# Output projection with stationary weights and 256 moving tokens; a second layer that takes turned sums

## The chip, the core and the metric

The kernel is one program on one core of a Trainium2 chip. TensorE (PE) multiplies matrices, VectorE (DVE), ScalarE (ACT) and GpSimd (POOL) work on elements, and SyncE (SP) issues the transfers (DMA). Every engine takes its instructions in order from a queue of its own, and waits where one needs what another engine or a transfer has not yet done. The metric is the device time in microseconds; lower is better. A measurement of a kernel here is the median of several runs.

## The reference

Input x is 4 x 256 tokens of 512 columns in float32, handled as 1024 tokens. It goes through three layers, each added to x:

```python
x = L0_attn_hidden_states
x = x + 0.5 * _L0_ffn_ref(_layernorm(x, axis=-1), L0_ffn_A, L0_ffn_B, L0_ffn_Wr)
x = x + _L0_attn_ref(_layernorm(x, axis=-1), L0_attn_wq, L0_attn_wkv, L0_attn_wo)
x = x + 0.5 * _L0_ffn_ref(_layernorm(x, axis=-1), L0_ffn_A, L0_ffn_B, L0_ffn_Wr)
```

The attention has 32 heads and causal softmax, and ends in an output projection by `wo` (4096 x 512):

```python
attn = jnp.einsum('bhqk,bkhd->bqhd', probs, v).reshape(B, S, H * DV)
return jnp.einsum('bse,ed->bsd', attn, wo)
```

The feed-forward layer has 64 small experts of rank 16. Each token is routed to 16 of them:

```python
scores = xf @ Wr.T
top_vals, top_idx = jax.lax.top_k(scores, TOPK)
gates = jax.nn.softmax(top_vals, axis=-1)
G = jnp.zeros((N, K), xf.dtype).at[jnp.arange(N)[:, None], top_idx].set(gates)
h = jnp.einsum('nd,krd->nkr', xf, A)
out = jnp.einsum('nkr,kdr->nd', h * G[:, :, None], B)
```

The layernorm is (x − mean) / sqrt(var + 1e-5), with no weights. The same A, B and Wr serve both feed-forward layers.

## The kernel before

All products are in float32, which TensorE does as two records of the trace for each matmul instruction. To save products, every large matrix product is made by a scheme of Strassen's kind: a 2 x 2 block product is done with seven products (M1 to M7) instead of eight, of which four need sums of blocks on either side; the results are then added together. `left_sums` (L197) forms the left blocks' sums, `seven` runs the products with their reads.

Stages in order of time: the first feed-forward layer, the attention (16 groups p of two heads, eight units of one head and one batch each), the output projection, the second feed-forward layer "f2". x stays in SBUF throughout as a tile of 128 partitions x 8 token tiles x 512 columns, token within the tile on the partition.

**The projection** (`out_products`, L1312) uses the scheme on two levels. The outer one has seven products in the order M1, M2, M6, M5, M3, M7, M4, each in four parts of the inner dimension: 28 steps k. A step has 14 products, the seven inner ones for each of two groups g. For every k `load` (L1384, L1385) has SP fetch four raw blocks of the left operand (`ol`, attention outputs turned so that the inner dimension is on the partitions; 512 KB for each g) and of the right one (`or`, weights; 256 KB for each g), mostly three steps ahead; `sums` (L1391) forms the others on VectorE, four adds of 128x512 and four of 128x256; then each product is two matmuls of 128x128 (L1491), with 128 tokens stationary and 128 columns of the weights moving. A PSUM tile thus holds tokens on the partitions and columns along the free dimension. Steps 0 and 3 use operands held in pieces of their own (`o`). After every fourth step `read` (L1424, and one ACT copy, L1426) puts the seven accumulators together into `y` (seven adds of 128x256) and adds that, or a running `yu`, into the quarters of x (adds of 128x1024).

The projection's first products are spread among the last head groups' units; the driver at the end (from L1868 on) takes the rest one product at a time, 392 in all. At every 28th from 112 on it loads one of f2's seven `a` blocks, and at products 316 and 356 it lets f2 do a piece of its preparation.

**f2** goes over four pairs of token tiles. For a pair, `prepare` (L458) takes the layernorm's statistics (L111, L112), the root on ACT and the reciprocal on VectorE (L116, L117), normalizes on ACT (L137, `xn`), turns both tiles by eight TensorE transposes (L144, `ptx`), copies them to SBUF on ACT (L467, `fxT`), forms the four left sums (L197, `fxs`), makes the router's products (L367, `pr`) and the gates (`gate_of_one`, L431 to L455). `hidden` (L490, `ph`) makes h by seven products, read by L503 and L507 into `hg`; GpSimd multiplies by the gates (L521). `move` turns hg of the first three pairs in 32x32 blocks on VectorE (L534), sends the blocks through DRAM (L539, four DMAs for each of two tiles) and loads them back (L545); `turned` copies the result (ACT, L559) and forms the sums (VectorE, L570, `hs`). The last pair is turned by TensorE (L585). `back` (L604, `po`) makes the layer's output by seven products, and its reads (L616) add it to x; the store to DRAM is L1883. The loop runs hidden of pair u and then back of pair u − 1, with the preparation of pair u + 1 between.

Before the attention's end, each engine's order is written out by a list of due times (`written`, `later`), in units of TensorE's time. From the driver on, the order within each engine is set by a scheduler at build time from the program's order and dependences.

Of the kernel before, what the change touches and what calls it, by code (L numbers as in the profile page):

```python
# [14 lines left out]
P = 128  # L15
# [19 lines left out]
def macaron_kernel(  # L35
# [69 lines left out]
    def norm_stats(ts, name, whole=True):  # L105
# [3 lines left out]
        for j, t in enumerate(ts):  # L109
            st = small.tile([P, nc.vector.BN_STATS_DIM], F32, tag="st", name=f"st_{name}_{t}")  # L110
            tc.keep_in_program_order(nc.vector.bn_stats(out=st, in_=x[:, t, :]))  # L111
            nc.vector.bn_aggr(out=mv[:, j, :], in_=st)  # L112
# [188 lines left out]
    def ffn(name, pairs, a_sums, b_sums, after, late, aside=None, raw=None):  # L301


        with ExitStack() as scope:
# [123 lines left out]
            def gate_of_one(n, ps):  # L428

                sc = work.tile([P, E], F32, tag="sc", name=f"sc_{n}")  # L430
                nc.vector.tensor_copy(sc, ps[:, 0:E])  # L431
                top = work.tile([P, 8], F32, tag="top", name=f"top_{n}")
                nc.vector.max(out=top, in_=sc)
                left = work.tile([P, E], F32, tag="left", name=f"left_{n}")
                nc.vector.match_replace(
                    out=left, in_to_replace=top, in_values=sc, imm_value=TAKEN
                )
                top2 = work.tile([P, 8], F32, tag="top2", name=f"top2_{n}")
                nc.vector.max(out=top2, in_=left)
                left2 = work.tile([P, E], F32, tag="left2", name=f"left2_{n}")  # L440
                nc.vector.match_replace(
                    out=left2, in_to_replace=top2, in_values=left, imm_value=TAKEN
                )
                nmax = work.tile([P, 1], F32, tag="nmax", name=f"nmax_{n}")
                nc.vector.tensor_scalar_mul(nmax, top[:, 0:1], -1.0)
                ex = ps[:, E : 2 * E]
                nc.scalar.activation(ex, sc, AF.Exp, bias=nmax)
                gate = work.tile([P, E], F32, tag="gate", name=f"gate_{n}", bufs=4)
                den = work.tile([P, 1], F32, tag="den", name=f"den_{n}")
                nc.vector.scalar_tensor_tensor(  # L450
                    gate, left2, TAKEN, ex, ALU.is_equal, ALU.mult, accum_out=den
                )
                rden = work.tile([P, 1], F32, tag="rden", name=f"rden_{n}")
                nc.vector.reciprocal(rden, den)
                nc.scalar.mul(gate, gate, rden)  # L455
                return gate

            def prepare(pair):  # L458


                n = f"{name}_{pair[0]}"
                tokens = normed(work, pair, name)
                yield
                xt = work.tile([P, 2, DC, P], F32, tag="fxT", name=f"fxT_{n}")
                pt = [turned_x(tokens[i], f"{name}_{t}") for i, t in enumerate(pair)]
                for i in range(2):
                    nc.scalar.copy(xt[:, i], pt[i])  # L467
                xs = work.tile([P, 4, 2, P], F32, tag="fxs", name=f"fxs_{n}")
                left = left_sums(
                    nc.vector,  # L470
                    [xs[:, i] for i in range(4)],
                    *(xt[:, i, k : k + 2] for i in range(2) for k in (0, 2)),
                    pt[0][:, 0:2],
                    pt[0][:, 2:4],
                    xt[:, 1, 0:2],
                    pt[1][:, 2:4],
                )
                lefts.append(left)
# [3 lines left out]
                gated_by.append([gate_of_one(f"{name}_{t}", ps) for t, ps in zip(pair, scores)])  # L482
# [115 lines left out]
            def back(pair, left, b_right):  # L598
# [14 lines left out]
                def read(r, ps):  # L613
                    i, j, _ = READS[r]
                    to = x[:, pair[i], j * 256 : (j + 1) * 256]
                    nc.vector.tensor_tensor(to, to, ps[:, 0:256], ALU.add)  # L616
# [135 lines left out]
            else:  # L752
                tokens = ready(pairs[0])
                take(tokens, 1)
                yield
                take(tokens, 1)
                yield
                take(tokens, 1)
                a_right = a_sums()
            for u in () if late else range(n + 1):  # L760
                hid = hidden(pairs[u], lefts[u], hgs) if u < n else iter(())
                tokens = ready(pairs[u + 1]) if u + 1 < n else iter(())
# [3 lines left out]
                take(tokens, 1)  # L766
                take(hid, 2)
                take(tokens, 1)
                take(hid, 1)
                take(tokens, 1)  # L770
# [9 lines left out]
                if u < n:  # L780
                    gated(hgs[pairs[u]], gated_by[u], False)
                    if pairs[u] in by_dma:
                        take(move(pairs[u], hgs[pairs[u]]), 3)
                if u > 0:
# [242 lines left out]
    work = right_pool(attention, "work")  # L1027
    pairs = right_pool(attention, "pairs")
# [283 lines left out]
    def out_products():  # L1312
# [81 lines left out]
        def operand(k, n, g, t):  # L1394

            cols = slice(t * P, (t + 1) * P)
            if k in (0, 3):
                parts = tiles[k, g]
                return parts[t][:, L_AT[n]], parts[2][:, R_AT[n]]
            left, right = tiles[k]  # L1400
            return left[:, g, L_AT[n], cols], right[:, g, R_AT[n]]

        def block(i, j):
            return x[:, 4 * i : 4 * i + 4, j * 256 : (j + 1) * 256]

        def read(m, banks):

            if m == "M1":
                y = outer["pool"].tile([P, 4, 256], F32, tag="u", name="yu", bufs=1)
                outer["u"] = y  # L1410
            else:
                y = outer["pool"].tile([P, 4, 256], F32, tag="y", name=f"y_{m}", bufs=1)
# [545 lines left out]
```

## Time and profile before

| | us |
|---|---|
| median of 3 runs | 1111.73 (1111.62 to 1112.86) |
| the profiled execution, its own time | 1112.9 |
| its span | 1111.1 |
| granted TensorE clock | 1.0 |
| TensorE idle before, in the projection from 866.5 on | 0 |
| product L1491, records, busy | 1456, 165.0 |
| multiplications by the gates L521 on POOL, busy | 34.0 |
| start of the projection's last stretch on TensorE | 981.80 |
| end of the projection on TensorE (start of the router's products) | 997.88 |

The times of the trace count from the start of the span. A group of instructions stands under its source line, engine, operation and tile, with the number of records after an x. The duration of a single matmul record includes its latency, since matmuls overlap; what one costs in a full stream is read from the distance of two groups' starts. The chain of waits follows the last instruction back from cause to cause. The DMA issues have the median time from issue to landing.

### The profile page before, as it was taken

Reading aid. Unit: us, or ns where it says so; the run is one execution under the profiler, and the core shown is the slowest. Engines: PE = TensorE matmul, PEld = TensorE weight load, DVE = VectorE, ACT = ScalarE, POOL = GpSimd, SP = SyncE. Lnnn points to the kernel's source line nnn. Section 1 sums busy time; section 2 is a strip of 40 time slices with the busy share of each in tenths; the row PEclk is TensorE's granted clock in tenths of the full one; section 3 lists DMA queues with packets and bytes.
Section 4 is the critical chain, followed back from the end, with each engine's and each line's share of the span. In section 5 each row is a group of like instructions: output and inputs, shape, how many; then the busy total and the mean of one; then the engine's idle time right before and its main releaser. Section 6 shows DMA issues by size and latency. Waiting matters only on the chain.

```text
span 1111.1 us, 20951 instructions
## 1 busy us (share of the span) xinstructions
PE 1098.3 (99%) x6742; PEld 968.0 (87%) x6742; DVE 823.4 (74%) x2238; ACT 427.6 (38%) x1306; POOL 631.4 (57%) x877
## 2 busy tenths in 40 slices
PE   8999999999999999999999999999999999999998
PEld 5776888899999999999999999999899999995667
DVE  6655776778778778778778778878778978866543
ACT  2234334444544544544544544544442000106410
POOL 3935587737887887797788788788532000002120
PEclk9999999999999999999999999999999999999999
DMA  9412121057757656656756656755798998752331
GB/s 314 183 32 83 32 65 30 18 147 206 199 147 202 198 142 186 207 152 177 211 147 189 202 149 183 201 163 164 215 315 304 343 342 259 257 193 76 95 95 39
DMA packets 204638, 190.55 MB, mean 171 GB/s; under 512 B 74224, under 2 KB 166384, under 8 KB 204272
## 3 DMA queue, kind: packets, MB, share of 16 engines
q1 hardware_dynamic: 204528, 189.21, 56.5%
q8 instruction: 54, 0.88, 0.3%
q14 instruction: 56, 0.46, 0.1%
HBM read 119.28 MB, written 69.86 MB: 170 GB/s over the span
## 4 chain that ended last, share of the span: by engine, by line
PE 86%; DVE 5%; DMA 4%; POOL 3%; ACT 1%; issue 1%; SPq 1%; POOLq 0%; DVEq 0%
PE po_M L1491 12%; PE pqk_c L1067 9%; PE pqk_b L1067 8%; PE po_f L604 8%; PE pqk_d L1067 7%; PE ph_f L490 7%; PE pv_c L1166 5%; PE ps L1516 5%; PE pa L1592 4%; PE pqk_a L1067 4%; PE pv_b L1166 4%; PE ps L1515 2%; PE pa L1599 2%; PE pv_d L1166 2%; PE pv_a L1166 2%; PE pv_e L1166 2%
## 5 line engine op out<-in xcount | busy, mean ns | idle before, releaser
L521 POOL TENSOR_TENSOR hg_f<-hg_f,gate_f 128x512 f32<-128x512 f32 x32 | 34.0, 1078 | 232.9 <-ACT gate_f L455 151.8
L1491 PE MATMUL po_M<-or_M,ol_M 128*128 128x128 f32 x1456 | 165.0, 275 | 0.7 <-DVE or_M L1391 0.7
L1491 PEld LDWEIGHTS po_M<-or_M,ol_M 128*128 128x128 f32 x1456 | 163.8, 192 | 1.0 <-DVE or_M L1391 0.9
L911 POOL TENSOR_TENSOR wqk_M<-wqk_M 128x128 f32<-128x128 f32 x320 | 142.3, 459 | 12.1
L911 POOL TENSOR_TENSOR wqk_M<-wqk_M,wqk_M 128x512 f32<-128x512 f32 (+1 forms) x64 | 107.2, 1685 | 46.4 <-DMA wqk_M<-in_wkv 25.1
L1084 DVE TENSOR_TENSOR qk<-qk,pqk_d 128x512 f32<-128x512 f32 x210 | 116.3, 558 | 21.9 <-PE pqk_d L1067 18.0
L1536 ACT ACTIVATE s<-s,least 128x128 f32<-128x128 f32 (+1 forms) x256 | 114.1, 448 | 41.2 <-DVE least L1524 38.0
L1554 ACT ACTIVATE pn<-s,arden 128x128 f32<-128x128 f32 x220 | 94.0, 427 | 47.8 <-DVE arden L1545 43.2
L1067 PE MATMUL pqk_c<-xop,wqk_M 128*128 128x256 f32 x448 | 111.4, 380 | 0.1
L1067 PE MATMUL pqk_d<-xop,wqk_M 128*128 128x256 f32 x420 | 108.2, 381 | 1.1 <-DVE qk L1084 1.1
L1067 PE MATMUL pqk_b<-xop,wqk_M 128*128 128x256 f32 x420 | 102.9, 379 | 0.0
L1391 DVE TENSOR_TENSOR ol_M<-ol_M 128x512 f32<-128x512 f32 x104 | 75.9, 730 | 23.5 <-DMA ol_M<-left 21.9
L1524 DVE CUSTOM_DVE_ANT_0 s<-ps,mask 128x128 f32<-128x128 f32 (+1 forms) x256 | 80.8, 353 | 16.1 <-PE ps L1516 12.4
L1084 DVE TENSOR_TENSOR qk<-qk,pqk_c 128x256 f32<-128x256 f32 (+1 forms) x112 | 59.4, 531 | 40.5 <-PE pqk_c L1067 36.5
L1084 DVE TENSOR_TENSOR qk<-qk,pqk_b 128x512 f32<-128x512 f32 x105 | 71.3, 679 | 20.7 <-PE pqk_b L1067 19.9
L1067 PEld LDWEIGHTS pqk_c<-xop,wqk_M 128*128 128x128 f32 x448 | 79.1, 191 | 8.7 <-ACT qk L1116 1.2
L1606 ACT COPY attn<-pa 128x256 f32<-128x256 f32 x128 | 47.5, 371 | 99.5 <-PE pa L1599 86.6
L1067 PEld LDWEIGHTS pqk_b<-xop,wqk_M 128*128 128x128 f32 x420 | 74.9, 191 | 7.5
L1067 PEld LDWEIGHTS pqk_d<-xop,wqk_M 128*128 128x128 f32 x420 | 73.0, 191 | 9.1 <-DVE qk L1084 2.9
L1592 PE MATMUL pa<-pT,vbuf 128*128 128x256 f32 x256 | 76.4, 380 | 1.5 <-DMA pT<-moved 1.0
L1516 PE MATMUL ps<-qk 128*128 128x256 f32 x256 | 76.5, 380 | 0.0
L911 POOL TENSOR_TENSOR wv_M<-wv_M 128x128 f32<-128x128 f32 x160 | 71.5, 461 | 5.0 <-DMA wv_M<-in_wkv 0.6
(221 smaller groups left out, 2344.1 us busy)
## 6 DMA issues: line engine op xcount, KB each, us to landing
ol_M<-left SPq DMA_DIRECT2D x52, 512.0 KB, 5.8
moved<-s SPq DMA_DIRECT2D x440, 48.0 KB, 1.8
pT<-moved SPq DMA_DIRECT2D x110, 192.0 KB, 2.9
wv_M<-in_wkv SPq DMA_DIRECT2D x64, 128.0 KB, 2.6
wqk_M<-in_wq SPq DMA_DIRECT2D x64, 128.0 KB, 2.3
wqk_M<-in_wkv SPq DMA_DIRECT2D x64, 128.0 KB, 2.5
wo<-in_wo SPq DMA_DIRECT2D x16, 512.0 KB, 4.7
left<-attn SPq DMA_DIRECT2D x16, 512.0 KB, 3.3
```

What stands on the lines that cost most here:

```text
L490: nc.tensor.matmul(ps, lhsT=left[m][:, c, :], rhs=a_right[m][:, c, :], start=first and c == 0, stop=c == 1, skip_group_check=True,)
L604: nc.tensor.matmul(ps[:, 0:256], lhsT=left[m][:, c, :], rhs=b_right[m][:, c, :], start=first and c == 0, stop=c == 3, skip_group_check=True,)
L911: return nc.gpsimd.tensor_tensor(to, a, b, ALU.subtract)
L1067: nc.tensor.matmul(ps[:, i * S : (i + 1) * S], lhsT=right[m][n], rhs=xop[OUTER[m]][:, INNER[n]], start=first and i == 0, stop=True, skip_g ...
L1084: nc.vector.tensor_tensor(to, of, ps, ALU.add)
L1166: nc.tensor.matmul(ps[:, i * S + t * P : i * S + (t + 1) * P], lhsT=xop[OUTER[m]][:, INNER[n], t * P : (t + 1) * P], rhs=right[m][n], star ...
L1491: nc.tensor.matmul(banks[at // 2][:, cols : cols + P], lhsT=lhsT, rhs=rhs, start=k % 4 == 0 and g == 0 and at % 2 == 0 and t == 0, stop=Tr ...
L1516: nc.tensor.matmul(ps[:, P : 3 * P], lhsT=qT[:, P : 2 * P], rhs=kT, start=True, stop=True)
L1524: nc.vector.tensor_tensor_reduce(out=s[:, cols], in0=ps[:, cols], in1=mask_f[:, cols], scale=-SCALE, scalar=-TAKEN, op0=ALU.add, op1=ALU.m ...
L1536: nc.scalar.activation(s[:, cols], s[:, cols], AF.Exp, bias=least[:, i : i + 1], scale=-1.0, accum_out=den[:, i : i + 1],)
L1554: nc.scalar.mul(pn[:, :, i : 2 * i + 1, :].rearrange("p k t c -> p t k c"), s[:, cols].rearrange("p (t k c) -> p t k c", k=4, c=32), rden[ ...
L1592: nc.tensor.matmul(po[:, 0 : 2 * P], lhsT=v_of(p, j, 2 * b), rhs=of[:, 0:2], start=True, stop=False,)
```

## The change

Four things are changed.

1. In the projection, for all steps but 0 and 3, one product is one matmul with the right operand (weights, 128 columns) stationary and all 256 tokens moving. Steps 0 and 3 keep two matmuls of 128x128, with the sides exchanged as well. The accumulators then hold columns on the partitions and tokens along the free dimension, so `read` adds turned blocks.
2. So that these blocks can be added to x, the tokens of x are turned in 32x32 blocks in the attention stage: `turn_tokens`, once for each of the eight token tiles, in unit 1 of groups 2 to 9. VectorE transposes 128x512, four DMAs of 64 KB go out to DRAM and one of 256 KB comes back into x, on SP, at two due times.
3. `prepare` of f2 turns x back to plain tokens for the statistics and the later addition (`xp`, by a VectorE transpose of 128x1024, four DMAs of 128 KB and a load of 512 KB), takes the statistics of `xp`, sends the means to DRAM as a row of 256 numbers and loads that row back into all partitions, and subtracts it from the turned x on VectorE. The scale by the root is applied later, on the gates (`gates`, which the first layer already used, with 1/root formed on ACT and POOL). The TensorE transposes, the normalizing on ACT, the root and its reciprocal, and the ACT copies go away. Stages of all four pairs are called at new places: those of pairs 0 and 1 at ten products of the projection, those of pairs 2 and 3 in the loop, and the routing after three of the seven hidden products.
4. `back`'s first add for each part of x takes its other operand from `xp` (plain tokens) instead of x.

The smaller scratch area set where the program is built (`dynamic_dma_scratch_size`) changes no instruction.

```diff
@@ norm_stats
-    def norm_stats(ts, name, whole=True):
+    def norm_stats(ts, name, whole=True, of=x):
...
-            tc.keep_in_program_order(nc.vector.bn_stats(out=st, in_=x[:, t, :]))
+            tc.keep_in_program_order(nc.vector.bn_stats(out=st, in_=of[:, t, :]))
@@ prepare
-                tokens = normed(work, pair, name)
+                to = plain[pair] = work.tile([P, 2, D], F32, tag="xp", name=f"xp_{n}", bufs=4)
+                ts = slice(pair[0], pair[1] + 1)
+                blocks = work.tile([P, 2, D], F32, tag="xb", name=f"xb_{n}")
+                nc.vector.transpose(blocks, x[:, ts])
+                moved = scratch.tile([2, P, 4, P], F32, tag="moved_p", name=f"moved_{n}", bufs=4)
+                for q in range(4):
+                    nc.sync.dma_start(
+                        moved[:, :, q].rearrange("i (k r) x -> r (i k) x", r=32),
+                        blocks[32 * q : 32 * q + 32].rearrange("r i (k x) -> r (i k) x", k=4),
+                    )
+                yield
+                nc.sync.dma_start(to, moved.rearrange("i p q x -> p i (q x)"))
+                yield
+                mv, rstd = norm_stats((0, 1), n, None, to)
+                row = scratch.tile([1, 2 * P], F32, tag="mean", name=f"row_{n}", bufs=2)
+                nc.sync.dma_start(row.rearrange("o (i s) -> s (o i)", i=2), mv[:, :, 0])
+                mean = work.tile([P, 2 * P], F32, tag="mean", name=f"mean_{n}", bufs=2)
+                yield
+                nc.sync.dma_start(mean, row.broadcast_to([P, 2 * P]))
                 yield
                 xt = work.tile([P, 2, DC, P], F32, tag="fxT", name=f"fxT_{n}")
-                pt = [turned_x(tokens[i], f"{name}_{t}") for i, t in enumerate(pair)]
-                for i in range(2):
-                    nc.scalar.copy(xt[:, i], pt[i])
+                for i, t in enumerate(pair):
+                    nc.vector.tensor_tensor(
+                        xt[:, i].rearrange("p c (k r) -> p k c r", r=32),
+                        x[:, t].rearrange("p (k c r) -> p k c r", c=DC, r=32),
+                        mean[:, i * P : (i + 1) * P]
...
+                        ALU.subtract,
+                    )
...
+                lefts.append(left_of(xt, xs))
                 yield
                 for scores in route(pair, xt):
                     pass
-                gated_by.append([gate_of_one(f"{name}_{t}", ps) for t, ps in zip(pair, scores)])
+                for _ in gates(pair, scores, rstd):
+                    pass
@@ back, read
+                    if adds or late:
+                        nc.vector.tensor_tensor(to, to, of, ALU.add)
+                        return
+                    to, of = (v.rearrange("p (c q r) -> p q c r", q=4, r=32) for v in (to, of))
+                    was = plain[pair][:, i].rearrange("p (q c r) -> p q c r", q=4, r=32)
+                    nc.vector.tensor_tensor(to, was[:, :, 2 * j : 2 * j + 2], of, ALU.add)
@@ the loop of f2
+                all_of = [ready(pair) for pair in pairs]
+                for u in (0, 1, 0, 1, 0, 1, 0, 1, 0, 1):
+                    take(all_of[u], 1)
+                    yield
...
                 take(hid, 1)
                 take(behind, 1)
-                take(tokens, 1)
+                if u == 0:
+                    take(all_of[2], 1)
+                    take(all_of[3], 1)
                 take(hid, 2)
-                take(tokens, 1)
+                if u < n:
+                    take(all_of[u], 1)
...
@@ out_products
         def block(i, j):
-            return x[:, 4 * i : 4 * i + 4, j * 256 : (j + 1) * 256]
+            of = x[:, 4 * i : 4 * i + 4].rearrange("p t (k c r) -> p c (t k) r", c=DC, r=32)
+            return of[:, 2 * j : 2 * j + 2]
...
-                for t in range(2):
+                weight, tokens = operands_of(k, n, g)
+                for t, rhs in enumerate(tokens):
                     cols = at % 2 * 256 + t * P
-                    lhsT, rhs = operand(k, n, g, t)
                     nc.tensor.matmul(
-                        banks[at // 2][:, cols : cols + P],
-                        lhsT=lhsT,
+                        banks[at // 2][:, cols : cols + S // len(tokens)],
+                        lhsT=weight,
                         rhs=rhs,
@@ turning x in the attention
+    def turn_tokens(t):
+
+        blocks = turned_pool.tile([P, D], F32, tag="xb", name=f"xb_{t}", bufs=1)
+        nc.vector.transpose(
+            blocks.rearrange("p (q c r) -> p q c r", q=4, r=32),
+            x[:, t].rearrange("p (c q r) -> p q c r", q=4, r=32),
+        )
+        moved = scratch.tile([P, 4, P], F32, tag="moved_x", name=f"moved_x_{t}", bufs=2)
+        for k in range(4):
+            nc.sync.dma_start(
+                moved[:, k].rearrange("(q r) x -> r q x", r=32),
+                blocks[32 * k : 32 * k + 32].rearrange("r (q x) -> r q x", q=4),
+            )
+        yield
+        nc.sync.dma_start(x[:, t], moved.rearrange("p k x -> p (k x)"))
...
+        if unit == 1 and 2 <= p < 2 + NT:
+            moving = turn_tokens(p - 2)
+            later(t + 3.0, take, moving, 1)
+            later(t + 9.0, take, moving, 1)
@@ the driver
-        if step in (8 * 7 * 5 + 36, 8 * 7 * 6 + 20):
+        if step in (300, 305, 311, 317, 323, 328, 333, 336, 344, 350):
             next(second_layer)
```

## The prediction

> **What bounds the kernel now.** I read the engine table first, then the table of stretches, then the chain of waits and the order of TensorE at the places that the change touches, and last the durations on VectorE and the DMA issues. "Back to back" below means from one group's start to the next one's start.
>
> ```profile
> PE 1098.3 (99%) x6742; PEld 968.0 (87%) x6742; DVE 823.4 (74%) x2238; ACT 427.6 (38%) x1306; POOL 631.4 (57%) x877
> ...
> 800.00:866.40 66.40, 64.09 (x520) 61.55 (x518) 53.30 (x151) 22.82 (x75) 16.34 (x12) 1.00 0.92 314
> 866.50:998.00 131.50, 131.50 (x1178) 131.50 (x1179) 104.78 (x220) 6.88 (x15) 0.00 (x0) 1.00 0.84 279
> 998.00:1029.30 31.30, 31.27 (x121) 17.26 (x119) 21.02 (x93) 20.54 (x39) 6.96 (x7) 1.00 0.25 68
> 1029.40:1111.00 81.60, 78.22 (x320) 56.86 (x320) 37.03 (x89) 19.46 (x34) 10.45 (x10) 1.00 0.27 78
> ```
>
> In the stretches the columns after the length are busy PE, weight loads, DVE, ACT, POOL, the granted clock, the DMA share and GB/s. TensorE is never idle from 866.5 to 998 (131.50 of 131.50 at clock 1.00), almost never in the second layer's first part, and in its last part only at one wait and the tail. So what TensorE is spared there is time, unless a new wait appears. VectorE is the engine with least to spare in the projection (104.78 of 131.50).
>
> ```profile
> 866.43 114.65 PE L1491 MATMUL po_M<-or_M,ol_M 128*128 128x128 f32 x1024 [0.73 <-DVE or_M L1391]
> 980.92 1.04 PE L144 MATMUL ptx_f<-ident,xn_f 128*128 128x128 f32 x8
> 981.80 16.24 PE L1491 MATMUL po_M<-or_M,ol_M 128*128 128x128 f32 x144
> ...
> 1034.11 3.29 PE L604 MATMUL po_f<-b_f_M,hs_f 128*128 128x256 f32 x14 [0.23 <-DVE hs_f L570]
> ...
> 1104.40 1.89 PE L604 MATMUL po_f<-b_f_M,hs_f 128*128 128x256 f32 x8
> 1106.13 1.89 PE L604 MATMUL po_f<-b_f_M,hgT_f 128*128 128x256 f32 x8
> ```
>
> Every f32 product is two records. Back to back a 128x128 record costs (980.92 − 866.43)/1024 = 0.1118 us, a 128x256 one (1106.13 − 1104.40)/8 = 0.2163. The eight transposes of one pair cost 981.80 − 980.92 = 0.88.
>
> **Part 1, fewer and wider products.** 1456 records of 128x128 (the line's count in the table of groups) become 728 of 128x256; the 112 records of steps 0 and 3 stay. Each pair gives 2 × 0.1118 − 0.2163 = 0.0073. Not all of it counts:
>
> ```profile
> 804.95 8.13 DMA ol_M<-left
> ...
> 834.88 6.40 DMA left<-so
> 841.30 5.25 DMA or_M<-in_wo
> ...
> 863.69 0.70 DVE ol_M L1391
> ```
>
> The chain of waits runs from 804 to 866 over transfers, not TensorE, and ends in its 0.73 us wait at 866.43. The 288 records before (1456 − 1024 − 144) save 144 × 0.0073 = 1.05 us that I give back to that wait. From 866.43 on there are 1168 records: 584 × 0.0073 = **−4.3**. Lower end −5.3 (all counts); upper end 0, if the wide form here is no faster per column, for which only the nearest row, L604's, speaks.
>
> The skill has a rule that says less. The Trainium skill ("TensorE: Matmul & The Clock Gate", "Wait — 56ns, not 53.3ns?") gives each matmul a fixed cost of about 2.5 ns besides its columns. By that, 584 fewer records would give 1.5 us, by the rows 4.3; the rows are f32 in this kernel, so I go by them.
>
> **Part 2, no transposes on TensorE.** Four pairs by 0.87 to 0.88: **−3.5**. They lie in stretches with TensorE full; the third and fourth pair's could be swallowed by a later wait (upper end −1.7). With Part 1: −7.8.
>
> **Part 3, turning x in the attention stage.** Eight VectorE transposes of 128x512 and eight times five DMAs. The transpose of 128x1024 takes 1.24 (L534 in the groups on VectorE), so 0.62 each, 5 us in all, spread over eight heads' pairs where VectorE is at 37.12 of 45 us (215 to 260) and TensorE at 45.00. VectorE has 7.9 us spare per 45, so I take **+0.3**; 0 to 5 if the cover fails. On SP the 40 DMAs stand among the probabilities' transfers (0.46 to issue, 2.3 per tile). In the written order these go out 6.0 and 10.8 after their scores, and their product comes at 19.5; the second lands in 2.9 (pT<-moved), so some 5 us are to spare, more than 2.3. Next are the rows for the group on VectorE, then those of the DMA issues (KB each, median us from issue to landing).
>
> ```profile
> L534 DVE STREAM_TRANSPOSE hgB_f<-hg_f 128x1024 f32<-128x1024 f32 x6 | 7.5, 1242 | 4.2 <-POOL hg_f L521 4.2
> ```
>
> ```profile
> moved_f<-hgB_f SPq DMA_DIRECT2D x24, 128.0 KB, 2.4
> hg_f<-moved_f SPq DMA_DIRECT2D x6, 512.0 KB, 4.3
> ...
> out_x<-x SPq DMA_DIRECT2D x16, 128.0 KB, 1.7
> ```
>
> **Part 4, the mean row at the projection's end.** Call T the start of step 24. A step is 14 × 2 × 0.2163 = 6.06 us (was 6.26), so step 27 is due at T+18.2. VectorE first adds M7's accumulators (to T+0.5), then three x and u adds of 1.2, in between step 25's eight sums (0.60 and 0.34 back to back) and the statistics of pairs 0 and 1 (0.61 and 0.1 back to back): pair 0's end at T+8, pair 1's at T+9.7, step 25's last sum at T+10.6. TensorE does the products of raw blocks of steps 25 and 26 meanwhile and, by the order in which the changed kernel issues, does not wait. The adds into x and the subtracts now go in runs of 32; the only VectorE row with such runs is L534's, 1.24 per 1024 columns beside 1.2 for a plain add, so I price them as plain. POOL, idle here (0.00 in the stretch), takes the four powers. SP's queue then reads: row of pair 0, row of pair 1, one of step 27's four loads, mean of pair 0, mean of pair 1, the other three loads. The row is 256 pieces of 4 bytes. No row of before has such pieces; nearest in size is the fastest, out_x at 1.7, and the slowest in this stage is b_f_M<-kept_b at 8.4. I take 2.4, the row of the blocked moved_f. Pair 1's row is issued at T+9.7 and lands at T+12.1; its mean load is issued then, the three loads of step 27 at T+12.6 to 13.6, and at 5.5 us (ol_M and or_M in this stage) they land at T+18.1 to 19.1. TensorE wants the first at T+18.2. VectorE, in order, does step 26's sums to T+14.4, waits for pair 1's mean to T+15, subtracts (four of 0.6) and makes eight left sums (0.35) among step 27's own sums, the last of which is done at T+23.4; four records of hidden of pair 0 stand inside step 27 and cover that. So a wait of 0 to 2, taken as **+1.0**. Behind it on TensorE stands the whole second layer.
>
> On the pieces the skill speaks against the change. The Trainium skill ("DMA: Bandwidth & Descriptors", "Specifications") puts full rate at 512 B or more and a read-modify-write below. No run here shows what 4 bytes cost; by that rule the row would lie nearer the slow end, and the sum nearer the third rival below.
>
> **Part 5, the second layer.** E is the projection's end. Before, back of pair 0 began at 1029.39, 31.5 after E, with 0.5 us of waits around 1034. Now hidden of pair 0 ends at E+12.1 (24 records, 10.36 in the chain of waits, four more being inside step 27, and 1.73 of routing), hidden of pair 1, with 28, at E+25.9. Back of pair 0 wants its first turned half then. Its way: gating and two transposes to E+16, eight DMAs (0.46 each, 2.4 to land) to E+20.5, and two loads of hg, the second of which stands on SP behind the row of pair 2, which waits for that pair's statistics. Those stand on VectorE after the gates of pair 1, at about E+23. On ACT the first copy of 1.03 stands behind pair 3's rstd, about E+25. Start of back E+26.4 to E+28. The second copy, at E+29, and the sums (0.6 each), behind pair 2's subtract and so behind its mean load, then come just in time. Over the 0.5 of before: **+1.7** (0 to 4). Later pairs have a whole hidden and back stage, 26 us, of cover, and the tail (last x add 0.42, stores 1.7) is the same. The table loads, ACT's xn and the copies that go away ran beside a full TensorE: nothing.
>
> **The sum.** Against the profiled execution's span: 1111.1 − 4.3 − 3.5 + 0.3 + 1.0 + 1.7 = 1106.3. That execution took 1112.9, 1.8 more than its span, but the median of the runs is 1111.73, 0.6 above the span; so **1106.9 us**. With Parts 4 and 5 at their ends: 1104.2 (0 and 0) to 1110.2 (2 and 4), its own range.
>
> **The rivals.** *No new wait shows* (17%). For it: the rows of 128 KB in the second layer land in 1.7 to 2.4 us and the loads of the projection have one step to spare. Then 1111.7 − 7.8 = 1103.9, and 1102.9 with the 1.05 before 866 kept. Against: step 27's loads stand behind two round trips.
>
> *The gain is given back* (16%): the row lands 4 to 6 us after its issue, or the wide products give none of their 4.3 (1111.2 then). Time 1109.5 to 1113.9. For it: a second order on SP that waits on statistics; against: TensorE's rows.
>
> *Slower by the mean's round trip* (17%). One price, the landing time L of the row, counts at two places: step 27's loads behind pair 1's mean on SP, and pair 2's mean ahead of back's sums on VectorE. Both waits grow one for one past 2.4: 1.0 + 1.7 + 2(L − 2.4). Slower begins where they exceed 7.8 − 0.3 + 2.2 = 9.7, at L = 5.9; at the slow row, 8.4, they are 14.7 and the time 1111.7 − 7.8 + 0.3 + 14.7 = 1118.9. For it: order on queues; against: the moves in short pieces of before land early, moved<-s in 1.8, pT<-moved in 2.9.
>
> **How the numbers follow.** Forecast 50%, rivals 17, 16 and 17. A measurement of this kernel tells 0.2% from none, 2.2 us: faster is under 1109.5, slower over 1113.9. Faster 0.66, same 0.17, slower 0.17. The range 1102.8 to 1113.0 leaves the slower rival out.
>
> **What would show it.** po_M at 0.216 per 128x256 record; no ptx_f; the row's landing in the list of DMA issues near 2.4 and the wait of po_M at step 27 under 2; the wait of po_f before back of pair 0 about 2; TensorE's stretches in attention as full as now. I am wrong if the row lands late, if VectorE's sums of steps 25 to 27 leave TensorE idle, or if turning x costs the attention stage more than 1 us.

## The result, and the profile after

| | before | after |
|---|---|---|
| median, 6 runs each (us) | 1112.07 (1111.62 to 1112.86) | 1129.53 (1127.46 to 1130.79) |
| ratio to before, 95% interval | | 1.0156 [1.0143, 1.0169] |
| profiled execution: its time, its span | 1112.9, 1111.1 | 1129.56, 1127.8 |
| granted TensorE clock | 1.0 | 0.989 |

The change costs 17.5 us; the prediction was 1106.9, in a range of 1102.8 to 1113.0. TensorE does 760 records fewer (5982 instead of 6742), and its busy time is the same 1098.3. The order of TensorE in the profile after shows both halves of this. Columns: start, length, engine, line, records, and in brackets the idle time before them and what ended it.

```profile
864.15 112.49 PE L1496 MATMUL po_M<-ol_M,or_M 128*128 128x256 f32 x518 [0.43 <-DVE or_M L1395]
977.13 8.47 PE L1496 MATMUL po_M<-ol_M,or_M 128*128 128x256 f32 x38 [0.49 <-DVE or_M L1395]
992.09 2.04 PE L1496 MATMUL po_M<-ol_M,or_M 128*128 128x256 f32 x4 [6.49 <-DMA or_M<-right]
995.61 2.05 PE L1496 MATMUL po_M<-ol_M,or_M 128*128 128x256 f32 x4 [1.47 <-DMA or_M<-right]
...
1000.40 4.48 PE L1496 MATMUL po_M<-ol_M,or_M 128*128 128x256 f32 x20
1004.72 1.88 PE L478 MATMUL ph_f<-a_f_M,fxT_f 128*128 128x512 f32 x4
...
1032.71 5.41 PE L592 MATMUL po_f<-b_f_M,hgT_f 128*128 128x256 f32 x16 [1.94 <-ACT hgT_f L547]
1045.58 7.47 PE L592 MATMUL po_f<-b_f_M,hs_f 128*128 128x256 f32 x20 [7.46 <-DVE hs_f L558]
1052.89 1.89 PE L592 MATMUL po_f<-b_f_M,hgT_f 128*128 128x256 f32 x8
```

Up to 977 all is as meant: the stream starts at 864.15 (866.43 before), and 112.49/518 gives 0.2172 a record, for what were two records of 0.1118. Then come two stretches of waiting that before doesn't have: 6.49 + 1.47 us for the weights of step 27, and 1.94 + 7.46 us in back of pair 0. The chain of waits names what was late; its columns are start, length and what ran or was in flight.

```profile
977.20 10.45 DMA row_f<-mv_f
...
987.67 0.34 SPq L451
988.00 0.05 issue
988.05 0.43 SPq L1389
...
990.02 5.45 DMA or_M<-right
...
1029.05 9.51 DMA row_f<-mv_f
1038.56 0.02 issue
1038.57 5.63 DMA mean_f<-row_f
1044.20 0.02 issue
1044.23 0.69 DVE fxT_f L455
1044.92 0.61 DVE hs_f L558
```

Both times it is the row of means, 1 KB, in flight for 10.45 and 9.51 us. At 977 the last three loads of step 27 (L1389, then L1388 and L1389 again) stand on SP behind the mean (L451), which waits for the row. At 1029 the subtract of pair 2 (L455) waits for its mean, and the sums of back (L558) stand behind it on VectorE. The DMA issues of the stretch 950 to 1060 (KB each, median us from issue to landing) set it beside a transfer of the same stretch with 128 times the bytes:

```profile
moved_f<-hgB_f SPq DMA_DIRECT2D x16, 128.0 KB, 3.7
...
mean_f<-row_f SPq DMA_DIRECT2D x4, 128.0 KB, 4.9
...
row_f<-mv_f SPq DMA_DIRECT2D x4, 1.0 KB, 10.0
```

There is a second loss, which the waits don't list: the records that follow them are slow. After 1032.71, 16 records take 12.87 − 7.46 = 5.41 us where 3.46 is the rule (16 × 0.2163); after 1045.58, 20 take 7.31 where 4.33 is. The table of stretches shows the clock there (after the length: busy PE, weight loads, DVE, ACT, POOL, then the granted clock, the DMA share and GB/s).

```profile
864.00:976.00 112.00, 111.76 (x516) 97.95 (x517) 96.09 (x196) 2.16 (x6) 0.08 (x1) 1.00 0.89 300
...
992.00:1001.00 9.00, 7.44 (x15) 4.43 (x16) 8.17 (x20) 0.77 (x2) 0.00 (x0) 0.56 1.00 354
...
1046.00:1054.00 8.00, 8.00 (x26) 6.10 (x26) 7.21 (x18) 0.00 (x0) 0.00 (x0) 0.68 0.79 276
```

The clock is 1.00 in the full stream and on average 0.56 and 0.68 behind the two waits. Busy time hides it: from 1046 to 1054 TensorE counts as busy for 8.00 of 8.00 us.

The account of the spans: waits 8.0 and slow records 3.4 before 1004.72 (from 992.09 on 12.63, less a wait of 1.47, for 28 records of 0.2163 and four of 0.43); waits 9.4 and slow records 4.9 in back of pair 0 (1.95 and 2.98); a wait of 0.8 at 1096. That is 26.5, less 0.9 for what back of pair 0 had lost before. Against it stand the gains, 5.0 from the wide products by the projection's end (below) and 3.5 from the transposes. 25.6 − 8.5 = 17.1; the spans differ by 16.7.

### The profile page after: what moved, and what is told of

It is laid out like the page before. It is cut to its first block, busy times and chain, and to the rows that moved or that the text cites. A ratio compares the mean times of both kernels' runs of the same rounds, so it can differ in the third digit from the quotient of the medians.

```text
span 1127.8 us, 19482 instructions
## 1 busy us (share of the span) xinstructions
PE 1098.3 (97%) x5982; PEld 944.5 (84%) x5982; DVE 837.1 (74%) x2254; ACT 409.1 (36%) x1278; POOL 633.4 (56%) x881
## 4 chain that ended last, share of the span: by engine, by line
PE 82%; DMA 7%; DVE 5%; POOL 2%; SPq 1%; ACT 1%; issue 1%; DVEq 0%; POOLq 0%
PE po_f L592 8%; PE pqk_c L1071 8%; PE pqk_b L1071 8%; PE po_M L1496 8%; PE pqk_d L1071 7%; PE ph_f L478 7%; PE ps L1521 5%; PE pa L1597 4%; PE pv_c L1170 4%; PE pqk_a L1071 4%; PE pv_b L1170 4%; DMA ol_M<-left 2%; PE ps L1520 2%; PE pa L1604 2%; PE pv_a L1170 2%; PE pv_d L1170 2%
## 5 line engine op out<-in xcount | busy, mean ns | idle before, releaser
L1496 PE MATMUL po_M<-ol_M,or_M 128*128 128x256 f32 x728 | 162.5, 383 | 9.0 <-DMA or_M<-right 8.0
L1496 PEld LDWEIGHTS po_M<-ol_M,or_M 128*128 128x128 f32 x728 | 138.0, 191 | 30.3 <-issue 7.1
L120 POOL TENSOR_TENSOR rstd_f<-rstd_f,halves 128x2 f32<-128x2 f32 x8 | 5.6, 704 | 128.1 <-ACT rstd_f L119 128.1
```

What stands on the lines that cost most here:

```text
L1496: nc.tensor.matmul(banks[at // 2][:, cols : cols + S // len(tokens)], lhsT=weight, rhs=rhs, start=k % 4 == 0 and g == 0 and at % 2 == 0 an ...
```

## The experiments

Each is an edit of the changed kernel, three of them together with the first one below. The kernel before, run beside them, had medians of 1112.35, 1112.15 and 1112.12 (16, 30 and 12 runs). Line numbers of the profiles move by a few from one kernel to the next.

### The row in 8 pieces

VectorE turns the column of means in a 32x32 block transpose, so that four DMAs of two times 128 bytes make the row. Its place in SP's queue stays.

```diff
+flat = work.tile([P, 32], F32, tag="flat", name=f"flat_{n}", bufs=2)
...
+nc.vector.tensor_copy(flat[:, 0:2], mv[:, :, 0])
+nc.vector.transpose(flatT, flat)
-nc.sync.dma_start(row.rearrange("o (i s) -> s (o i)", i=2), mv[:, :, 0])
+to_row = row.rearrange("o (i q r) -> (o i) q r", i=2, q=4)
+for q in range(4):
+    nc.sync.dma_start(to_row[:, q], flatT[32 * q : 32 * q + 2, :])
```

> The changed kernel with the same row through DRAM at the same place in SP's queue, but first turned by a 32x32 transpose on VectorE, so that it leaves as 8 pieces of 128 bytes (four DMAs) in place of 256 pieces of 4. Theory 'row' lays the 10 us to the number of pieces: the row lands in 1.7 to 2.5 us, the waits fall to 0 to 2 and 0 to 3 us: 1106 to 1111. Rival 'crowding', or a price of any transfer to DRAM and back at this place: the row still lands after 8 us or more and the time stays above 1122.

Measured: 1109.76 (1108.88 to 1111.3, 8 runs), ratio 0.9974 [0.9964, 0.9984]; 19.8 us less than the change as it was, from the row alone. SP's order in this kernel (start, length of issuing, transfer):

```profile
977.20 2.61 SPq L455 DMA_DIRECT2D row_f<-flatT_f  x8
979.97 0.36 SPq L458 DMA_DIRECT2D mean_f<-row_f  x1
980.38 0.43 SPq L1395 DMA_DIRECT2D ol_M<-left  x1
980.97 0.34 SPq L458 DMA_DIRECT2D mean_f<-row_f  x1
981.35 0.43 SPq L1396 DMA_DIRECT2D or_M<-right  x1
```

The second pair's last DMA is issued from 979.56 to 979.81 (by the chain of waits), and its mean goes out at 980.97: the row is there within 1.4 us of its issue. (The profile gives no landing time for this row itself.) Step 27's last three loads go out from 981.35 on, not from 988. So the landing time of the row is the cause of nearly all the loss. What is left here are waits of 0.65 and 1.25 in the projection and one of 3.3 ahead of back of pair 0.

### What makes the row slow: number or size of its pieces

First, mean and variance are sent together, 128 pieces of 16 bytes. Then the same is written twice by one transfer: 256 pieces, as in the change, of 16 bytes.

```diff
-nc.sync.dma_start(row.rearrange("o (i s) -> s (o i)", i=2), mv[:, :, 0])
+nc.sync.dma_start(row.rearrange("o (s e) -> s (o e)", e=4), mv.rearrange("p i v -> p (i v)"))
...
-nc.sync.dma_start(row.rearrange("o (s e) -> s (o e)", e=4), mv.rearrange("p i v -> p (i v)"))
+nc.sync.dma_start(row.rearrange("o (s e) -> s o e", e=4),
+    mv.rearrange("p i v -> p (i v)").unsqueeze(1).to_broadcast([P, 2, 4]))
```

> The changed kernel (1129.5) with its row sent with the variances beside the means, as 128 pieces of 16 bytes in place of 256 of 4 (the loads of the mean are then of 256 KB, and VectorE reads every fourth number of it). Nothing else is moved. If the 10 us come from the number of pieces, the row lands after about 5 and both waits fall by 5: 1114 to 1121. If it is that pieces are short at all, it lands after 8 to 10: 1127 to 1131. If it is the 4 bytes alone, after 2 or 3: 1108 to 1113.

> Measures the landing time by itself. The row of mean and variance, 128 pieces of 16 bytes, which landed in 2.8 us, is written twice by one transfer: 256 pieces of 16 bytes. If the number of pieces sets the landing time: some 5.6 to 10 us, as far as the row of 256 pieces of 4 bytes, and the time goes above 1118. If the 4 bytes of a piece set it: 3 to 4 us, and the time stays at 1114 to 1117.

Measured: 1114.83 (1112.24 to 1116.43, 6 runs), ratio 1.0024 [1.0012, 1.0037]; and 1114.85 (1113.88 to 1116.4, 5 runs), ratio 1.0021 [1.0008, 1.0034]. The DMA issues, of the first and of the second:

```profile
row_f<-mv_f SPq DMA_DIRECT2D x4, 2.0 KB, 2.8
```

```profile
row_f<-mv_f SPq DMA_DIRECT2D x4, 4.0 KB, 3.2
```

256 pieces of 16 bytes land in 3.2 us, 256 of 4 bytes in 10.0. The number of pieces isn't it; pieces of 4 bytes are. Where between 4 and 16 bytes the step lies was not measured, and why 4 bytes are slow is not shown.

By its time the first of the two missed: its landing time is that of "the 4 bytes alone", but 1114.83 lies in the range given for the number of pieces. Both kernels differ in more than the row: the mean has one buffer in place of two, so pair 1's mean goes out only at 985.72 in the first, behind pair 0's subtracts, and a subtract, which now reads every fourth number, takes 1.05 us in place of 0.69. The longest waits left there, 2.46 in the projection and 2.99 in back of pair 0, are for VectorE.

### The place in the queues

The row stays slow, but pairs 0 and 1 ask for row and mean at products 338 to 341, when step 27's loads have been issued (at product 336, the first of step 24). In the trace all four loads then stand ahead of both rows on SP, and step 27's sums ahead of the subtracts on VectorE.

```diff
-if step in (300, 305, 311, 317, 323, 328, 333, 336, 344, 350):
+if step in (300, 305, 311, 317, 338, 339, 340, 341, 344, 350):
```

> The changed kernel with the row and the mean of pairs 0 and 1 asked for a little later, inside step 27's own products: step 27's four loads then stand ahead of both rows on SP, and its sums ahead of the subtracts on VectorE. The row itself is untouched, 256 pieces of 4 bytes. Theory (the first wait, 8.0 us and about 3.3 of low clock behind it, comes only from step 27's loads standing behind rows that land 10 us after their issue): it goes but for 1 or 2 us, the wait ahead of back of pair 0 stays at 7 to 10 us with its low clock; 1118 to 1122. Rival (the wait only moves, because step 27's left operands or hidden of pair 0 need the mean anyway): the wait shows up at the last products of step 27 or at hidden of pair 0, and the time stays at 1127 or above.

Measured: 1121.25 (1119.53 to 1121.75, 4 runs), ratio 1.0075 [1.006, 1.0091]. TensorE's order:

```profile
976.76 14.51 PE L1496 MATMUL po_M<-ol_M,or_M 128*128 128x256 f32 x66 [0.49 <-DVE or_M L1395]
991.11 1.88 PE L478 MATMUL ph_f<-a_f_M,fxT_f 128*128 128x512 f32 x4
995.29 3.34 PE L478 MATMUL ph_f<-a_f_M,fxT_f 128*128 128x512 f32 x4 [2.30 <-DVE y_M L1429]
...
1037.52 7.72 PE L592 MATMUL po_f<-b_f_M,hs_f 128*128 128x256 f32 x20 [7.03 <-DVE hs_f L558]
```

The projection now ends without a stop, with one of 2.30 behind it, in hidden of pair 0, where the rival had it, and a little longer than the theory's 1 or 2; the wait in back stays, 7.03. So the two places are separate, and the first was worth 8.3 us (1129.53 − 1121.25). The same move on the row in 8 pieces:

> The same move on top of the row that leaves in 8 pieces. Theory: the waits that this kernel still had at the end of the projection (1.2 for a load, 0.65 for VectorE) go, the 3.3 us ahead of back of pair 0 stays; 1107.5 to 1109. Rival (what is taken from there comes back as a wait for hidden of pair 0): 1109.8 as without the move, or more.

Measured: 1108.23 (1107.38 to 1109.82, 5 runs), ratio 0.9964 [0.9952, 0.9977]. The waits in the projection are two of 0.6, the 3.3 ahead of back is still there. This was the fastest kernel of all, ahead of before by 3.9 us.

### The mean without a transfer

The mean is spread over the partitions by TensorE, as a diagonal matrix times ones, two records of 128x256 per pair; row and mean DMAs go. The stages of pairs 0 and 1 from the mean on are asked for 8 to 14 products later.

```diff
-nc.sync.dma_start(mean, row.broadcast_to([P, 2 * P]))
+nc.scalar.mul(diag[:, i], ident, many[:, i : i + 1])
+nc.tensor.matmul(mean[:, 0 : 2 * P].rearrange("p (j t) -> p j t", j=2),
+    lhsT=every, rhs=diag, start=True, stop=True)
...
-if step in (300, 305, 311, 317, 323, 328, 333, 336, 344, 350):
+if step in (300, 305, 311, 317, 323, 328, 344, 350, 352, 358):
```

> The changed kernel (1129.5) with the mean row's two transfers taken out: a diagonal matrix of the means times a matrix of ones on TensorE puts the means into PSUM, four matmuls of 128x256 (0.43 each), and VectorE subtracts from there. Theory 'row' (the row of 256 four-byte pieces lands after 10 us; step 27's loads stand behind it on SP, back's sums behind it on VectorE): both waits go, and with them the low clock after them: 1105 to 1109. Rival 'crowding' (transfers of the projection's end are late because too many move at once; the row is only one of them): step 27's loads still come late, 1115 to 1125. Rival 'wide form' (the products with 256 tokens or turning x cost time themselves): above 1112.

Measured: 1115.45 (1112.92 to 1116.83, 7 runs), ratio 1.0027 [1.0016, 1.0038]. No wait over 0.5 us is left in the projection, as expected; but at back of pair 0 there are 2.02 for the diagonal (ACT) and 4.02 for VectorE, and slow records behind both. The expectation missed these. In the next kernel the last pair's preparation was moved out of there, into hidden of pair 2:

> The kernel with the means by TensorE (1115.5), with the last pair's statistics, means and sums asked for in hidden of pair 2, behind back of pair 0. Theory 'queues' (that kernel lost its time at back of pair 0, where it waited 0.3, 2.0 and 4.0 us for VectorE and ACT, which did the last pair's work first; its projection ended 2 us sooner than that with the row in 8 pieces): these waits fall to 0 to 2.5 in all and the time to 1104 to 1108, below both kernels. Rival (means by TensorE cost the time themselves): 1112 or more.

Measured: 1111.85 (1109.79 to 1113.06, 11 runs), ratio 1.0000 [0.9991, 1.0008]. Missed again. VectorE's order there:

```profile
1023.90 2.37 DVE L528 STREAM_TRANSPOSE hgB_f<-hg_f 128x1024 f32<-128x1024 f32 x2
1026.19 0.65 DVE L564 TENSOR_TENSOR hs_f<-hgT_f 128x512 f32<-128x512 f32 x1
```

Back's sums (L564) stand behind the two block transposes of pair 1 (2.37), which nobody needs yet, though ACT's copies that they read are done at 1022.65; TensorE waits 3.68 us, until the add behind the sums (L615). The profile is of the fastest of the eleven runs, 1109.79, and the only one with a mean clock of 1.00; the others list 0.997 or 0.998, so the median has slow records besides.

### The last pair asked for later, with the row in 8 pieces

```diff
-                take(all_of[3], 1)
-            if 0 < u < n - 1:
-                take(all_of[u + 1], 1)
+            if u == 1:
+                take(all_of[2], 1)
...
+            if u == 1:
+                take(steps, 3)
+                take(all_of[3], 3)
```

> The kernel with the row in 8 pieces (1109.8), with the statistics, row and mean of the last pair asked for during back of pair 0 in place of before it. Theory 'queues' (back of pair 0 waits because the last pair's root stands ahead of pair 0's copies on ACT): its wait falls from 3.3 us to about 1.8, the clock falls less, and the time is 1106.5 to 1108.5. Rival (the wait is due to pair 0's own way through DRAM): 1109 to 1110.5.

Measured: 1110.56 (1106.76 to 1113.94, 12 runs), ratio 0.9984 [0.9973, 0.9995]. By its time it missed; it lies at the upper end of the rival's. The wait for ACT's first copy falls from 3.3 to 1.69, as the theory had it, and a wait of 2.96 for VectorE's sums follows. This time it isn't the block transposes, which end at 1027.83. ACT's and VectorE's orders:

```profile
1028.83 1.04 ACT L554 COPY hgT_f<-hg_f 128x1024 f32<-128x1024 f32 x1 [2.65 <-DMA hg_f<-moved_f]
```

```profile
1029.91 0.69 DVE L565 TENSOR_TENSOR hs_f<-hgT_f 128x512 f32<-128x512 f32 x1 [2.08 <-ACT hgT_f L554]
```

The sums wait for ACT's second copy, and that for the second load of hg of pair 0, which goes out at 1025.39. On SP it stands behind the first piece of pair 2's row (1024.98), which waits for that pair's statistics, as Part 5 of the prediction says. So pair 0's own way through DRAM is next, which was the rival. As one wait goes, the next in line shows; nothing is gained that can be told from the spread of the runs. The profile is of the slowest of the twelve.

### The wide products alone

Projection and turned x as in the change; f2 prepared as before, with `xn` on ACT and eight transposes on TensorE for each pair, and the last pieces of pairs 0 and 1 are asked for 8 and 10 products later. It leaves out one thing: the columns of `xp`, which come in the order of the turned blocks, are not put back into their own order, so its second layer's products take them in the wrong order.

```diff
-nc.sync.dma_start(mean, row.broadcast_to([P, 2 * P]))
+nc.scalar.activation(xn, to[:, j], AF.Identity, bias=bias, scale=rstd)
...
+pt = [turned_x(made[i], f"{name}_{t}") for i, t in enumerate(pair)]
```

> The wide projection and the turned x of the change, but f2's preparation as before on the plain tokens: normalized on ACT, turned by TensorE; no mean row. Theory 'row': the gain of the wide products shows without the loss: 1111.9 less 4.3 to 6.6, plus 0 to 2 for crowding on VectorE: 1105 to 1110. Rival 'wide form': 1112 or more.

Measured: 1117.07 (1115.14 to 1119.37, 6 runs), ratio 1.0039 [1.0026, 1.0052]. The projection runs through to 993.81, 1.76 of it two pairs' transposes: 992.05. Before ended at 997.88 with one pair's 0.87: 997.01. So the wide products give 5.0 us there, by one execution of each. The 3.7 of cheaper records in it (584 × 0.0064) is steady; the rest is an earlier start, and the start of the last 518 records differs from 863.8 to 867.7 among four profiles of kernels that are alike up to there. The expectation was missed: the time is in the rival's range, though not for the rival's reason. The whole is slower than before by a wait of 3.3 for pair 2's left sums and one of 1.6 for ACT's copy ahead of back of pair 0, with the clock at 0.50 from 1026 to 1036.

### The clock

In the changed kernel, idle products (their results unused) were put into both waits of back:

```diff
+if u == 1:
+    outer["fill"](4, "b")
+    take(steps, 2)
+    outer["fill"](16, "c")
```

> The changed kernel with idle products (ones times the router's weights, into an unused PSUM bank) put on TensorE into the two waits of back of pair 0: 4 before its first product, 16 before its third, 8.7 us in all, where 9.4 are waited. Theory 'clock' (the granted clock falls because TensorE idled): the clock stays near 1 there and the 36 records after the waits, which take 12.7 us in place of 7.8, take 8 to 9: 1124.5 to 1126.5. Rival (the clock falls for another reason, or the waits alone are the loss): 1129 to 1131.

Measured: 1133.24 (1131.25 to 1133.91, 4 runs), ratio 1.0182 [1.0167, 1.0198]; missed. The 16 records behind the covered first wait take 3.55 us, but the second wait became longer (12.9 us with the filler in it, for 7.46; it ends with an add into x, L609): 5.85 us stay idle behind the filler, and the 16 after it take 5.56. On the time this run decides nothing. The test was repeated on the row in 8 pieces, where one wait of 3.3 is to be filled, with seven products:

> The kernel with the row in 8 pieces (1109.8), with seven idle products (ones times the router's weights, into an unused PSUM bank; 3.0 us) put on TensorE into the one wait of 3.3 us that it has ahead of back of pair 0. Nothing else is moved, and the idle products compute nothing that is used. Theory 'clock' (a wait of some us makes the granted clock fall, and the 16 records after it take 5.1 us in place of 3.5): the clock stays at 1.00 and the kernel gets faster by about 1.6 us, to 1108.2. Rival (the low clock has another cause, or the products after the wait are slow because of their operands): 1109.8 or more.

Measured: 1109.50 (1108.56 to 1111.03, 10 runs), ratio 0.9979 [0.997, 0.9988]. Stretches of the row in 8 pieces without the filler, then of this kernel, then its TensorE order:

```profile
1020.00:1026.00 6.00, 2.68 (x7) 1.39 (x6) 5.60 (x14) 2.71 (x5) 3.59 (x5) 0.86 0.26 90
```

```profile
1020.00:1026.00 6.00, 5.70 (x27) 4.70 (x26) 5.42 (x12) 2.97 (x5) 2.54 (x4) 1.00 0.29 100
```

```profile
1019.84 3.19 PE L1925 MATMUL fill_b<-wr_sb,every 128*128 128x256 f32 x14
1023.32 3.72 PE L599 MATMUL po_f<-b_f_M,hgT_f 128*128 128x256 f32 x16 [0.30 <-ACT hgT_f L554]
1028.20 3.72 PE L599 MATMUL po_f<-b_f_M,hs_f 128*128 128x256 f32 x16 [1.16 <-DVE x L616]
```

With TensorE kept busy the clock is 1.00, and the 16 records take 28.20 − 1.16 − 23.32 = 3.72 instead of 5.10. All ten runs list a mean clock of 1.00, against two of the eight without the filler. That the slow records come from the idle time is so shown. The time does not follow (0.26 of the 1.6 us, and nothing by the ratios to before, 0.9979 and 0.9974): VectorE isn't ahead any more, and 1.16 us of waiting takes the place.

The traces also say when a wait is enough. The granted clock has two values, 1.00 and 0.50, and changes on a grid of 3.41 us: in the change as it was it is 0.50 for 10.24 us from 989.69 on, for 3.41 from 1034.06 and for 10.24 from 1040.89. Windows of that grid, in the change as it was and then in the means by TensorE with the last pair later (columns as above):

```profile
1030.65:1034.06 3.41, 1.47 (x7) 1.22 (x7) 3.08 (x4) 1.82 (x3) 2.20 (x3) 1.00 1.06 86
1034.06:1037.47 3.41, 3.41 (x9) 2.72 (x9) 0.00 (x0) 0.00 (x0) 0.00 (x0) 0.50 1.15 23
```

```profile
1023.90:1027.31 3.41, 1.58 (x8) 1.04 (x6) 3.38 (x5) 0.00 (x0) 0.00 (x0) 1.00 0.36 71
1027.31:1030.73 3.42, 1.57 (x7) 1.42 (x8) 2.21 (x5) 0.00 (x0) 0.00 (x0) 1.00 1.05 261
```

The wait of 1.94 lies in one window, and the next window is at 0.50. The wait of 3.68 is divided by an edge into 1.83 and 1.85, and the clock stays. Over the twelve profiles in which the clock changes at all, the 24 windows at 1.00 in which TensorE was idle for 1.91 us or more were each followed by one at 0.50, and none of the others, with 1.85 or less, was. A window at 0.50 was followed by another one if TensorE was idle in it for 0.79 us or more, and by 1.00 at 0.40 or less. One window at 0.50 costs a busy TensorE half of 3.41, about the 1.6 us above.

## Why the prediction failed

**The step that failed** is Part 4's price of the row: "nearest in size is the fastest, out_x at 1.7, and the slowest in this stage is b_f_M<-kept_b at 8.4. I take 2.4, the row of the blocked moved_f." It measured 10.0, above both. The rows that it was picked from move pieces of 1 KB and more (256 numbers for moved_f); none had pieces of 4 bytes, and those are what cost (10.0 against 3.2 for as many of 16 bytes, and at most 1.4 for 8 of 128). The choice went by the transfer's kind and bytes; the piece was the one quantity with no row near it. The Trainium skill's line on this ("DMA: Bandwidth & Descriptors", "Specifications": full rate from 512 B, read-modify-write below) pointed the right way. It does not tell 128 or 16 bytes from 4, and here these are the difference.

**The rival on the slower side was right in place and form.** It put the price on step 27's loads behind the mean on SP and on back's sums behind pair 2's mean, with waits of 1.0 + 1.7 + 2(L − 2.4). At L = 10.0 that is 17.9; the profile has 8.0 + 1.9 + 7.5 = 17.4. That the two places count one by one is shown by the move of the rows: 8.3 us for the first.

**A term that no step had**, so that it stood at nothing: the granted clock after a wait. The rival's sum at L = 10.0 gives 1111.7 − 7.8 + 0.3 + 17.9 = 1122.1; the slow records of 3.4 + 4.9 = 8.3 us make up the rest to 1129.5, with about 1 to spare.

**Part 1**, −4.3: right. The records cost 0.2172, so 584 of them save 3.7; with the earlier start of the stream the gain is 5.0. That the 1.05 us given back to the wait at 866 were not lost is likely (the stream starts 2.3 earlier in these two profiles), but the start differs by more than that between executions.

**Part 2**, −3.5: in line with the account, which closes to 0.4 us; not tried by itself.

**Part 3**, +0.3: it cost nothing that can be seen. From 200 to 600, where the eight transposes lie (260.8 to 558.1), TensorE is busy for 399.56 of 400 us, before and after. The transposes take 0.70 each (0.62 was priced); the VectorE adds in runs of 32 take 1.14 to 1.22, as priced.

**Part 5**, +1.7 for back of pair 0: the chain was right, the size too small. With the fast row the chain there is the one that the prediction names: pair 3's statistics on VectorE, its root on ACT, then ACT's first copy and TensorE. Its wait is 3.3, and 1.6 of slow records follow.

**With the row fast the time is in the stated range, but not at the point:** 1109.76 is 2.9 over it, and among the times of the rival by which the gain is given back. Of that, 0.9 is from the projection (1.9 of waits for 1.0), 1.1 from back (3.3 for 2.2) and 1.6 from the clock, less 0.7 from Part 1. That this closes to nothing is luck: the medians compared are from different sessions, and by the spans of the profiled executions the excess is 1.8 (1108.1 for 1106.3).

What stays open is how much of the 8.5 can be kept. The best kernel keeps 3.9 (1108.23). What stands in the way is back of pair 0; the runs show its next waits one behind the other (ACT's first copy; then the sums, behind block transposes or behind the second load of hg), but no kernel here had both out of the way.

## What to carry to other kernels

In these runs the size of its pieces priced a small transfer, not its bytes and not their number: where the profile has no row with such pieces, its landing time is an open term, and what stands behind it on an in-order queue should be moved, or the row turned on an engine first. A wait on TensorE can cost more than its length, since the records behind it may run at a lower clock; busy time won't show that, but records per microsecond and the granted clock will. Where several engines are just in time for one stage, taking one wait away shows the next, so its size is not the gain.

## What the runs showed of the chip

- 1 KB to DRAM in 256 pieces of 4 bytes: 10.0 us to land (median of four; 8.6 and 9.7 in two more kernels); 4 KB in 256 of 16 bytes: 3.2; 2 KB in 128 of 16 bytes: 2.8; 1 KB in 8 of 128 bytes: within 1.4.
- The granted clock is 1.00 or 0.50 and changes on a grid of 3.41 us. In these profiles it fell after every window of that grid in which TensorE was idle for 1.91 us or more, and after none with 1.85 or less. So the length of a wait alone doesn't tell: of four waits of 1.94 to 1.95 three left 16 records slow (5.2 to 5.4 us instead of 3.46) and the fourth, of which an edge cut off 0.14, did not; one of 3.68, in halves on two windows, left 16 in 3.55. The Trainium skill ("TensorE: Matmul & The Clock Gate", "Part 1: The HAM clock gate (the "warmup" mystery)") tells of half the clock after an idle window of some 3.4 us that runs freely. The two values and the window agree; that the window has to be idle throughout does not, 1.91 us of it were enough here.
